# Weighted values of a small attention summed on TensorE instead of VectorE, in pairs of tiles

## The chip, the cores and the metric

The kernel runs on one core of one Trainium2 chip. The metric is the device time of one execution in microseconds; several runs are taken and their median counts. One further execution is recorded by the hardware profiler, and everything said of engines and waits comes from that one.

Engines by the profile's names: PE is TensorE's matmul side and PEld its weight loads, DVE is VectorE, ACT is ScalarE, POOL is GpSimd, SP is SyncE, whose queue issues plain DMAs.

## The reference, cut to what matters

The program is four layers on a residual stream `x` of 4 batches x 1024 tokens x 128 channels. Each layer is half a feed-forward, an attention-like part, and the other half of the feed-forward, each on a layer norm of `x`. In layer 0 the feed-forward is a mixture of 8 experts, of which each token takes the best 2. Its attention does not run over tokens: it runs over the 16 heads of one token.

```python
x = x + 0.5 * _L0_ffn_ref(_layernorm(x), ...)           # experts, top 2 of 8
x = x + _L0_attn_ref(_layernorm(x), Wq, Wk, Wv, Wfc)
x = x + 0.5 * _L0_ffn_ref(_layernorm(x), ...)
...
# _L0_attn_ref, h = 16 heads of hd = 8
scores = einsum('bshd,bstd->bsht', Q, K) / sqrt(hd)     # s: token; h, t: heads
attn = softmax(scores, axis=-1)
out = einsum('bsht,bstd->bshd', attn, V).reshape(b, s, dm)
return out @ Wfc.T
```

For each token that is a 16 x 16 table of scores, a softmax along `t`, and 16 x 8 sums of 16 products with the values.

## The kernel before, in words

The residual stays on chip, channels on the 128 partitions, one tile `X[b]` of 1024 columns per batch. A batch is cut into NT = 8 tiles of 128 tokens. Everything is float32.

**Layer 0's attention** is the generator `l0_attn` (L498 to L569). It first takes the squares and scales of the layer norm (L503 to L511). `projected(i)` (L513) multiplies one tile with the joined weights of q, k and v into a PSUM bank, tokens on the partitions, and ScalarE copies it, scaled per token, into `qkv` (L517). `weighed` (L520) makes, on VectorE, the 128 x 2048 products of q and k for all pairs of heads (L525), sums them over the 8 channels to 256 scores (L527), takes the largest per head (L529) and subtracts it (L530); ScalarE takes the exponential (L532). `summed` (L535) sums the exponentials (L537) and inverts the sums (L538), makes the 2048 products of weights and values (L542), sums them over the 16 positions to 128 outputs (L544) and scales these (L545). The values' weight columns were put in the order (channel, head) on the host (L130), so that L542 and L544 read the positions one after another. TensorE then turns the tile (L562), channels back on the partitions, ScalarE copies it into `oS` (L563), and after four tiles one matmul with `wfc` goes into a bank that VectorE adds to `X` (L567 to L569).

The loop (L549 to L569) runs one tile ahead: the projection two tiles ahead, the scores one tile ahead of the sums.

**What runs beside it.** `experts` (L424) handles a block of 128 tokens of one expert at a time: SyncE's queue loads the weights `e_w` (L455), GpSimd gathers the tokens (L457), TensorE turns them (L461), VectorE copies them (`e_x`, L463), TensorE makes four matmuls, each followed by ScalarE's activation (`e_h`, L468), then four more, VectorE adds the bias (`e_y`, L441), and GpSimd scatters the rows (L442). A group of two batches has 39 blocks, a group of one batch 23. `route` (L276) sorts tokens to experts, with a chain of small VectorE instructions; `combine` (L476) gathers an expert group's results into the residual; `l1_ffn` is the next layer's feed-forward. All matmuls go through the helper `mm`, whose line is L227.

**What sets the order.** Each of these is a generator that yields a cost, in a planner's microseconds. `lanes` (L1182) always advances the lane with the lowest clock; this decides the order in which the program is written down. The attention yields 4 after its norm, 6 after the first scores, and 11.2 per tile; an expert block yields 2.6. Layer 0 is called with three lanes (`macaron`, L1202): one with experts and their routing, one with the attentions of batches 0 to 3 in turn and then the feed-forwards, one with late routing. An attention starts when the first experts of its batch are combined, and the second experts of batches 0 and 1 are routed when the attention of batch 1 is done. From that order the compiler draws up a fixed order for each engine, in which it may let a later instruction pass while an earlier one isn't ready; on the chip each engine then runs its queue in that order.

Tiles come from pools by tag: `qkv` has three buffers, `prod` three, the other tags two. PSUM has a pool of four banks for the expert lane and one of four for the others.

Of the kernel before, what the change touches and what calls it, by code (L numbers as in the profile page):

```python
# [13 lines left out]
ALU = mybir.AluOpType  # L14
AX = mybir.AxisListType

P = 128
B, S, D = 4, 1024, 128
NH, HD = 16, 8
NE, FC = 8, 4  # L20
NT = S // P
# [87 lines left out]
def _col(v):  # L109
    return np.asarray(v).reshape(-1, 1)  # L110


def _moe_pack(w1, w2, b1, b2):

    w2 = w2.reshape(FC, P, NE, D).transpose(1, 2, 0, 3).reshape(P, NE, FC * D)
    b1 = b1.reshape(NE, FC, P).transpose(2, 0, 1)
    return np.concatenate([w1, w2, b1, np.broadcast_to(b2, (P, NE, D))], 2)


def _packs(i):  # L120

    bc = np.broadcast_to

    l0m = [
        ("w", _moe_pack(
            i["L0_ffn_w1"].transpose(2, 0, 1), i["L0_ffn_w2"].transpose(2, 0, 1), i["L0_ffn_b1"], i["L0_ffn_b2"]
        ))
    ]
    l0s = [("rw", i["L0_ffn_router_w"].T)]
    wv = i["L0_attn_Wv"].T.reshape(D, NH, HD).transpose(0, 2, 1).reshape(D, D)  # L130
    l0a = [
        ("wqkv", np.concatenate([i["L0_attn_Wq"].T, i["L0_attn_Wk"].T, wv], 1)),
        ("wfc", i["L0_attn_Wfc"].T),
    ]

    l1f = [
        ("wg", i["L1_ffn_w_gate"].T),
        ("wu", i["L1_ffn_w_up"].T),
        ("wd", i["L1_ffn_w_down"].T.reshape(HIDC, P, D).transpose(1, 0, 2)),
    ]  # L140

    w = i["L1_attn_w_qkv"]
    turned = [2 * d + 1 if d < HD // 2 else 2 * d - HD for d in range(HD)]

    heads = lambda w, order: w.reshape(P, NH, HD)[..., order].reshape(P, D)
    straight = list(range(HD))
    l1a = [
        ("wq", heads(w[:, :D], straight)),
        ("wqt", heads(w[:, :D], turned)),
        ("wk", heads(w[:, D : 2 * D], straight)),  # L150
        ("wkt", heads(w[:, D : 2 * D], turned)),
        ("wv", w[:, 2 * D :]),
        ("wo", i["L1_attn_w_out"]),
        ("bo", _col(i["L1_attn_b_out"])),
    ]

    l2m = [
        ("w", _moe_pack(
            i["L2_ffn_w1"].transpose(1, 0, 2), i["L2_ffn_w2"].transpose(1, 0, 2), i["L2_ffn_b1"], i["L2_ffn_b2"]
        ))  # L160
    ]
# [17 lines left out]
    a = {k[8:]: v for k, v in i.items() if k.startswith("L3_attn_")}  # L179
    at = np.arange(P)  # L180
    turn = at % NH * HD + at // 32 + at % 32 // NH * 4
    l3a = [
        ("maa", np.concatenate([_col(a["time_maa_" + x]) for x in "xwkvrg"], 1)),
        ("w1", a["time_maa_w1"]),
        ("w2", a["time_maa_w2"][:4].reshape(P, D)),
        ("w2l", a["time_maa_w2"][4]),
        ("td", _col(a["time_decay"])),
        ("dw1", a["time_decay_w1"]),
        ("dw2", a["time_decay_w2"]),
        ("u", _col(a["time_faaaa"])),  # L190
        ("wr", a["W_r"]),
        ("wk", a["W_k"]),
        ("wv", a["W_v"][:, turn]),
        ("wg", a["W_g"][:, turn]),
        ("wo", a["W_o"][turn]),
        ("lng", _col(a["ln_gamma"][turn])),
        ("lnb", _col(a["ln_beta"][turn])),
    ]
    return {
        **_constants(),  # L200
        "l0m": l0m, "l0s": l0s, "l0a": l0a, "l1f": l1f, "l1a": l1a,
        "l2m": l2m, "l2s": l2s, "l2a": l2a, "l3f": l3f, "l3a": l3a,
    }


class Macaron:
# [291 lines left out]
    def l0_attn(self, ps, wp, m, b):  # L498
        nc = self.nc
        v = nc.vector  # L500
        X = self.X[b]
        scale = 1.0 / math.sqrt(HD)
        bank = lambda shape=(P, HALF): self.t(ps, list(shape), "bank")  # L503
        sq = self.t(wp, [P, S], "sq", bufs=1)
        for h in range(2):
            c = slice(h * HALF, (h + 1) * HALF)
            cen = bank()
            self.mm(cen, self.c0["center"], X[:, c])
            nc.scalar.activation(sq[:, c], cen, AF.Square)
        r = self.scales(ps, wp, sq, "a")  # L510
        yield 4  # L511

        def projected(i):  # L513
            pq = bank((P, 3 * D))
            self.mm(pq, X[:, i * P : (i + 1) * P], m["wqkvc"])
            qkv = self.t(wp, [P, 3, D], "qkv", bufs=3)
            nc.scalar.mul(qkv.rearrange("p a b -> p (a b)"), pq, r[:, i : i + 1])  # L517
            return qkv

        def weighed(qkv):  # L520
            q = qkv[:, 0, :].rearrange("p (h d) -> p h d", d=HD)
            k = qkv[:, 1, :].rearrange("p (t d) -> p t d", d=HD)
            sh = [P, NH, NH, HD]
            pr = self.t(wp, sh, "prod", bufs=3)
            v.tensor_tensor(pr, q.unsqueeze(2).to_broadcast(sh), k.unsqueeze(1).to_broadcast(sh), ALU.mult)  # L525
            sc = self.t(wp, [P, NH, NH], "sc")
            v.tensor_reduce(sc, pr, AX.X, ALU.add)  # L527
            mx = self.t(wp, [P, NH, 1], "mx")
            v.tensor_reduce(mx, sc, AX.X, ALU.max)  # L529
            v.tensor_tensor(sc, sc, mx.to_broadcast([P, NH, NH]), ALU.subtract)  # L530
            ex = self.t(wp, [P, NH, NH], "ex")
            nc.scalar.activation(ex, sc, AF.Exp, scale=scale)  # L532
            return ex

        def summed(qkv, ex):  # L535
            sm = self.t(wp, [P, NH, 1], "sm")
            v.tensor_reduce(sm, ex, AX.X, ALU.add)  # L537
            v.reciprocal(sm, sm)  # L538
            values = qkv[:, 2, :].rearrange("p (d t) -> p d t", d=HD)
            sh = [P, NH, HD, NH]  # L540
            pv = self.t(wp, sh, "prod", bufs=3)
            v.tensor_tensor(pv, ex.unsqueeze(2).to_broadcast(sh), values.unsqueeze(1).to_broadcast(sh), ALU.mult)  # L542
            o = self.t(wp, [P, NH, HD], "o")
            v.tensor_reduce(o, pv, AX.X, ALU.add)  # L544
            v.tensor_tensor(o, o, sm.to_broadcast([P, NH, HD]), ALU.mult)  # L545
            return o.rearrange("p h d -> p (h d)")


        qkvs = [projected(0), projected(1)]  # L549
        exs = [weighed(qkvs[0])]  # L550
        yield 6
        for i in range(NT):
            if i + 2 < NT:
                qkvs.append(projected(i + 2))
            if i + 1 < NT:
                exs.append(weighed(qkvs[i + 1]))
            k = i % 4
            if k == 0:
                oS = self.t(wp, [P, HALF], "oS")
            o = summed(qkvs[i], exs[i])  # L560
            oT = bank((P, P))
            nc.tensor.transpose(oT, o, self.c0["ident"])  # L562
            nc.scalar.copy(oS[:, k * P : (k + 1) * P], oT)  # L563
            yield 11.2
            if k == 3:
                y = bank()
                self.mm(y, m["wfc"], oS)  # L567
                c = slice((i - 3) * P, (i + 1) * P)
                v.tensor_tensor(X[:, c], X[:, c], y, ALU.add)  # L569


# [774 lines left out]
```

## Time and profile before

| | us |
|---|---|
| median of 3 runs | 3334.71 (3332.87 to 3340.66) |
| the profiled execution | 3264.24 |
| its span, first to last instruction | 3262.4 |
| mean granted TensorE clock | 0.909 |
| layer 0's attention, batch 0 to 3: first product (L525) to last addition (L569), start times | 151.9 to 264.7, 278.8 to 387.9, 413.4 to 539.9, 560.7 to 681.0 |
| VectorE busy, 0 to 955 us | 557.0 |
| TensorE matmul busy, 0 to 955 us | 712.6 |

Three kinds of view are used. The page has the busy share of each engine and cuts the span into 40 equal slices; a digit is the busy share of a slice in tenths, and PEclk the granted TensorE clock in tenths of full speed. A view by windows gives busy microseconds per engine and, in brackets, the number of instructions in each stretch of time. A view by groups puts instructions of one line, operation and shape together: busy us and mean ns of one stand after the bar, then the engine's idle time just before them and what it waited for. Ends of matmuls are modelled and matmuls overlap, so that a sum of their durations is larger than the time that they take; the distance from one to the next is what counts. A float32 matmul appears as two instructions, a transpose as one.

### The profile page before, as it was taken

The numbers are of one execution on the slowest core, as the hardware profiler recorded it, in microseconds if no ns is written. First come the engines' busy times: TensorE is split into PE (matmuls) and PEld (weight loads), VectorE is DVE, ScalarE is ACT, GpSimd is POOL, SyncE is SP. The second block draws the span as 40 slices with busy tenths as digits, with TensorE's granted clock in tenths as the row PEclk, the third lists the DMA queues.
The fourth block names the chain that finished last, engine by engine and source line by source line (L and its number), as shares of the span: only waits on it lengthen the run. The fifth ranks groups of instructions, "written<-read, shape, count | busy, mean of one in ns | idle before, by whom it ended". The sixth has DMA issues, their size and how long they took to land. (4 is left out here: it accounts for less than half of the span.)

```text
span 3262.4 us, 48511 instructions
## 1 busy us (share of the span) xinstructions
PE 2850.0 (87%) x18206; PEld 1660.8 (51%) x18206; DVE 1820.2 (56%) x3156; ACT 1640.6 (50%) x3632; POOL 805.4 (25%) x748
## 2 busy tenths in 40 slices
PE   7777748679879999999999998998988978899997
PEld 6656547556633333333333333586867867334433
DVE  3487786853245775776676771433546521355664
ACT  4556526667404665665565664464433545344442
POOL 2466407433340000000000000064523545010110
PEclk9888959889869999999999998898988989788997
DMA  5655516644400000000000000176644757000000
GB/s 179 193 178 185 168 46 199 183 121 136 152 13 3 6 6 4 6 5 5 17 6 4 1 1 12 47 232 183 200 119 130 217 169 238 13 1 1 7 7 13
DMA packets 122891, 277.64 MB, mean 85 GB/s; under 512 B 18017, under 2 KB 67297, under 8 KB 122529
## 3 DMA queue, kind: packets, MB, share of 16 engines
q1 hardware_dynamic: 101792, 231.77, 23.7%
q0 software_dynamic: 20864, 42.77, 4.2%
q8 instruction: 144, 2.36, 0.3%
q14 instruction: 91, 0.74, 0.1%
HBM read 238.43 MB, written 31.85 MB: 83 GB/s over the span
## 5 line engine op out<-in xcount | busy, mean ns | idle before, releaser
L717 DVE TENSOR_REDUCE nm<-two 128x2 f32<-128x1024 f32 x512 | 626.8, 1224 | 289.9 <-PE s L227 270.5
L740 ACT ACTIVATE e<-s 128x512 f32<-128x512 f32 x1024 | 555.8, 594 | 404.1 <-PE s L227 401.3
L468 ACT ACTIVATE e_h<-bank,e_w 128x128 f32<-128x128 f32 x1304 | 454.6, 368 | 460.9 <-PE bank L227 432.5
L227 PE MATMUL bank<-e_x,e_w 128*128 128x128 f32 x2608 | 560.9, 312 | 110.4 <-DVE e_x L463 43.4
L227 PE MATMUL s<-qm,kz 32*128 32x512 f32 x2048 | 634.2, 643 | 0.8 <-ACT e L740 0.8
L227 PE MATMUL two<-kz,qz 32*128 32x512 f32 x2048 | 593.2, 664 | 19.3 <-DVE nm L717 2.5
L457 POOL DMA_INDIRECT e_xg<-rows,g_source x326 | 336.8, 1033 | 876.8 <-DVE g_target L412 346.6
L227 PEld LDWEIGHTS bank<-e_x,e_w 128*128 128x128 f32 x2608 | 401.8, 197 | 238.1 <-ACT e_h L468 94.7
L442 POOL DMA_INDIRECT res<-e_y,g_target x326 | 369.5, 1134 | 282.9 <-DVE e_y L441 147.8
L227 PE MATMUL bank<-e_w,e_h 128*128 128x128 f32 x2608 | 435.4, 284 | 4.0 <-ACT e_h L468 2.3
L227 PEld LDWEIGHTS bank<-e_w,e_h 128*128 128x128 f32 x2608 | 366.3, 197 | 15.2 <-ACT e_h L468 11.6
L227 PE MATMUL o<-e,va 128*32 128x256 f32 x4096 | 328.6, 392 | 0.1
L441 DVE TENSOR_TENSOR e_y<-bank,e_w 128x128 f32<-128x128 f32 x326 | 94.0, 289 | 386.6 <-PE bank L227 380.5
L227 PEld LDWEIGHTS two<-kz,qz 32*128 32x128 f32 x2048 | 159.6, 189 | 237.8 <-issue 161.3
L227 PEld LDWEIGHTS o<-e,va 128*32 128x32 f32 x4096 | 81.0, 108 | 390.3 <-issue 371.1
L227 PEld LDWEIGHTS s<-qm,kz 32*128 32x128 f32 x2048 | 206.8, 183 | 11.0 <-issue 7.7
L705 POOL COPY va<-vd 128x256 f32<-128x256 f32 x16 | 6.7, 433 | 624.5 <-PE o L227 538.1
L1109 POOL TENSOR_TENSOR z<-st,r 128x512 f32<-128x512 f32 x32 | 46.2, 1444 | 403.3 <-DVE st L1102 240.3
L493 PE MATMUL bank<-c,c_y 128*128 128x128 f32 x128 | 39.3, 450 | 106.2 <-DVE c_y L490 106.2
L463 DVE COPY e_x<-bank 128x128 f32<-128x128 f32 x326 | 92.0, 282 | 62.1 <-PE bank L461 60.3
L461 PE MATMUL bank<-c,e_xg 128*128 128x128 f32 x326 | 93.2, 286 | 7.8 <-DMA e_xg<-rows,g_source 7.7
L227 PE MATMUL bank<-g_cols,g_lanes 128*128 128x39 f32 (+1 forms) x512 | 75.7, 303 | 24.4 <-DVE g_cols L392 24.4
(300 smaller groups left out, 3755.5 us busy)
## 6 DMA issues: line engine op xcount, KB each, us to landing
e_w<-in_l0m_dram SPq DMA_DIRECT2D x170, 578.0 KB
e_w<-in_l2m_dram SPq DMA_DIRECT2D x156, 578.0 KB
c_y<-res SPq DMA_DIRECT2D x32, 512.0 KB
rows<-g_xt SPq DMA_DIRECT2D x16, 512.0 KB
e_xg<-rows,g_source POOLq DMA_INDIRECT x326
res<-e_y,g_target POOLq DMA_INDIRECT x326
x<-in_x_dram SPq DMA_DIRECT2D x4, 512.0 KB
qz<-qd SPq DMA_DIRECT2D x64, 32.0 KB
```

What stands on the lines that cost most here:

```text
L227: self.nc.tensor.matmul(out, lhsT, rhs, start=start, stop=stop)
L441: nc.vector.tensor_tensor(y, o, w[:, MOE_W - D :], ALU.add)
L442: ins = nc.gpsimd.indirect_dma_start(out=res[:, :], out_offset=at(target[:, k : k + 1]), in_=y, in_offset=None)
L457: nc.gpsimd.indirect_dma_start(out=xg, out_offset=None, in_=rows[:, :], in_offset=at(source[:, k : k + 1]))
L461: nc.tensor.transpose(tp, xg, self.c0["ident"])
L463: nc.vector.tensor_copy(x, tp)
L468: nc.scalar.activation(h[:, fc, :], up[:, fc, :], func, bias=w[:, 2 * FC * P + fc : 2 * FC * P + fc + 1])
L493: nc.tensor.transpose(tp[:, j, :], y[1][:, i, :], self.c0["ident"])
L705: nc.gpsimd.tensor_copy(va[n % RING][:, :, :, 1 : 1 + HD], dense[b, "vd"][:, :, 32 * g4 : 32 * g4 + 32].rearrange("p t (h d) -> p t h d", ...
L717: v.tensor_reduce(nm[:, it, h, 2 * pair : 2 * pair + 2], s, AX.X, ALU.max, negate=True)
L740: nc.scalar.activation(es[g], s, AF.Exp, scale=scale)
L1109: (pool if i else v).tensor_tensor(z, st[:, 0:HALF], r, ALU.mult)
```

## The change

The attention of layer 0 is done for two tiles at a time, and the sum over positions moves to another engine.

- `projected` is as before, called for two tiles at a time; `qkv` gets six buffers instead of three. The values keep the order (head, channel).
- `weighed` takes a pair: products and sums of scores tile by tile as before, then the maximum, the subtraction and the exponential once for both tiles, over 512 elements.
- `summed` takes a pair: sum of exponentials and reciprocal once for both, then the exponentials themselves are scaled by it. For each tile VectorE makes the 2048 products, now with the position as outermost index. The sum over positions is 16 matmuls into one PSUM bank: the stationary operand is the 128 x 128 slice of products of a position, the moving operand the identity matrix, and the bank accumulates. The result is at the same time turned, so that the transpose falls away.
- ScalarE copies a pair's result in one instruction of 256 columns.
- The planner's costs become 9 after the scores of a following pair and 8 after the sums of a pair.

```diff
+        def weighed(pair):
+            sc = self.t(wp, [P, 2, NH, NH], "sc")
+            for j, qkv in enumerate(pair):
+                q, k = (qkv[:, n, :].rearrange("p (h d) -> p h d", d=HD) for n in range(2))
...
+                v.tensor_tensor(pr, q.unsqueeze(2).to_broadcast(sh), k.unsqueeze(1).to_broadcast(sh), ALU.mult)
+                v.tensor_reduce(sc[:, j], pr, AX.X, ALU.add)
+            mx = self.t(wp, [P, 2, NH, 1], "mx")
             v.tensor_reduce(mx, sc, AX.X, ALU.max)
+            v.tensor_tensor(sc, sc, mx.to_broadcast([P, 2, NH, NH]), ALU.subtract)
+            ex = self.t(wp, [P, 2, NH, NH], "ex")
             nc.scalar.activation(ex, sc, AF.Exp, scale=scale)
             return ex
...
-            v.tensor_tensor(pv, ex.unsqueeze(2).to_broadcast(sh), values.unsqueeze(1).to_broadcast(sh), ALU.mult)
-            o = self.t(wp, [P, NH, HD], "o")
-            v.tensor_reduce(o, pv, AX.X, ALU.add)
-            v.tensor_tensor(o, o, sm.to_broadcast([P, NH, HD]), ALU.mult)
-            return o.rearrange("p h d -> p (h d)")
+        def summed(pair, ex):
+            sm = self.t(wp, [P, 2, NH, 1], "sm")
             v.tensor_reduce(sm, ex, AX.X, ALU.add)
             v.reciprocal(sm, sm)
+            v.tensor_tensor(ex, ex, sm.to_broadcast([P, 2, NH, NH]), ALU.mult)
+            oT = bank((P, 2, P))
+            for j, qkv in enumerate(pair):
+                values = qkv[:, 2, :].rearrange("p (t d) -> p t d", d=HD)
+                sh = [P, NH, NH, HD]
+                pv = self.t(wp, sh, "prod", bufs=3)
+                v.tensor_tensor(
+                    pv, ex[:, j].rearrange("p h t -> p t h").unsqueeze(3).to_broadcast(sh),
+                    values.unsqueeze(2).to_broadcast(sh), ALU.mult,
+                )
+                for t in range(NH):
+                    self.mm(oT[:, j], pv[:, t].rearrange("p h d -> p (h d)"), self.c0["ident"], start=t == 0, stop=t == NH - 1)
+            return oT
...
+        pairs = [[projected(0), projected(1)]]
+        ex = weighed(pairs[0])
         yield 6
-        for i in range(NT):
...
-            yield 11.2
+        pairs.append([projected(2), projected(3)])
+        for n in range(NT // 2):
+            following = weighed(pairs[n + 1]) if 2 * n + 2 < NT else None
+            yield 9
+            if 2 * n + 4 < NT:
+                pairs.append([projected(2 * n + 4), projected(2 * n + 5)])
...
+            oT = summed(pairs[n], ex)
+            nc.scalar.copy(oS[:, n % 2 * 2 * P : (n % 2 + 1) * 2 * P], oT.rearrange("p i t -> p (i t)"))
+            ex = following
+            yield 8
```

More of the change, by code (lines that the diff above doesn't have):

```diff
@@ L129, in _packs @@
     l0s = [("rw", i["L0_ffn_router_w"].T)]
-    wv = i["L0_attn_Wv"].T.reshape(D, NH, HD).transpose(0, 2, 1).reshape(D, D)
     l0a = [
-        ("wqkv", np.concatenate([i["L0_attn_Wq"].T, i["L0_attn_Wk"].T, wv], 1)),
+        ("wqkv", np.concatenate([i["L0_attn_Wq"].T, i["L0_attn_Wk"].T, i["L0_attn_Wv"].T], 1)),
         ("wfc", i["L0_attn_Wfc"].T),
@@ L515, in projected @@
             self.mm(pq, X[:, i * P : (i + 1) * P], m["wqkvc"])
-            qkv = self.t(wp, [P, 3, D], "qkv", bufs=3)
+            qkv = self.t(wp, [P, 3, D], "qkv", bufs=6)
             nc.scalar.mul(qkv.rearrange("p a b -> p (a b)"), pq, r[:, i : i + 1])
             return qkv
[L520 to L528, printed above, removed]
+        def weighed(pair):
[3 more added lines that the diff above has]
+                sh = [P, NH, NH, HD]
+                pr = self.t(wp, sh, "prod", bufs=3)
+                v.tensor_tensor(pr, q.unsqueeze(2).to_broadcast(sh), k.unsqueeze(1).to_broadcast(sh), ALU.mult)
+                v.tensor_reduce(sc[:, j], pr, AX.X, ALU.add)
+            mx = self.t(wp, [P, 2, NH, 1], "mx")
@@ L529, in weighed @@
             v.tensor_reduce(mx, sc, AX.X, ALU.max)
-            v.tensor_tensor(sc, sc, mx.to_broadcast([P, NH, NH]), ALU.subtract)
-            ex = self.t(wp, [P, NH, NH], "ex")
+            v.tensor_tensor(sc, sc, mx.to_broadcast([P, 2, NH, NH]), ALU.subtract)
+            ex = self.t(wp, [P, 2, NH, NH], "ex")
             nc.scalar.activation(ex, sc, AF.Exp, scale=scale)
             return ex
-        def summed(qkv, ex):
-            sm = self.t(wp, [P, NH, 1], "sm")
+        def summed(pair, ex):
+            sm = self.t(wp, [P, 2, NH, 1], "sm")
@@ L537, in summed @@
             v.tensor_reduce(sm, ex, AX.X, ALU.add)
             v.reciprocal(sm, sm)
[L539 to L542, printed above, removed]
-            o = self.t(wp, [P, NH, HD], "o")
-            v.tensor_reduce(o, pv, AX.X, ALU.add)
-            v.tensor_tensor(o, o, sm.to_broadcast([P, NH, HD]), ALU.mult)
@@ L546, in summed @@
-            return o.rearrange("p h d -> p (h d)")
-        qkvs = [projected(0), projected(1)]
-        exs = [weighed(qkvs[0])]
-        yield 6
-        for i in range(NT):
[L553 to L558, printed above, removed]
-                oS = self.t(wp, [P, HALF], "oS")
[L560 to L563, printed above, removed]
-            yield 11.2
-            if k == 3:
+            v.tensor_tensor(ex, ex, sm.to_broadcast([P, 2, NH, NH]), ALU.mult)
@@ new lines, in summed @@
+            oT = bank((P, 2, P))
+            for j, qkv in enumerate(pair):
+                values = qkv[:, 2, :].rearrange("p (t d) -> p t d", d=HD)
+                sh = [P, NH, NH, HD]
+                pv = self.t(wp, sh, "prod", bufs=3)
[5 more added lines that the diff above has]
+                    self.mm(oT[:, j], pv[:, t].rearrange("p h d -> p (h d)"), self.c0["ident"], start=t == 0, stop=t == NH - 1)
@@ new lines, in summed @@
+            return oT
+        pairs = [[projected(0), projected(1)]]
+        ex = weighed(pairs[0])
+        yield 6
+        pairs.append([projected(2), projected(3)])
[4 more added lines that the diff above has]
+                pairs.append([projected(2 * n + 4), projected(2 * n + 5)])
+            if n % 2 == 0:
+                oS = self.t(wp, [P, HALF], "oS")
+            oT = summed(pairs[n], ex)
+            nc.scalar.copy(oS[:, n % 2 * 2 * P : (n % 2 + 1) * 2 * P], oT.rearrange("p i t -> p (i t)"))
+            ex = following
+            yield 8
+            if n % 2:
@@ L566, in l0_attn @@
                 y = bank()
                 self.mm(y, m["wfc"], oS)
-                c = slice((i - 3) * P, (i + 1) * P)
+                c = slice((n - 1) * 2 * P, (n + 1) * 2 * P)
                 v.tensor_tensor(X[:, c], X[:, c], y, ALU.add)
```

## The prediction

> **What bounds the kernel now.** I read the page first (shares, then slices), next the busy time by stage of layer 0, then the rows of the attention on VectorE, last the pace of single weight loads.
>
> ```profile
> PE 2850.0 (87%) x18206; PEld 1660.8 (51%) x18206; DVE 1820.2 (56%) x3156; ACT 1640.6 (50%) x3632; POOL 805.4 (25%) x748
> ...
> PE   7777748679879999999999998998988978899997
> ...
> DVE  3487786853245775776676771433546521355664
> ...
> PEclk9888959889869999999999998898988989788997
> ```
>
> A slice is 81.6 us. TensorE looks busy overall, but layer 0's attention lies in slices 2 to 8, where VectorE reads 6 to 8 and TensorE often no more. The stages follow from the attention's first and last instructions:
>
> ```profile
> core 0: us, PE busy (x) PEld busy (x) DVE busy (x) ACT busy (x) POOL busy (x), PEclk, DMA share, GB/s
> 143.70:397.00 253.30, 188.87 (x1157) 151.04 (x1155) 196.93 (x287) 154.19 (x352) 151.92 (x117) 0.91 0.58 175
> 397.00:481.00 84.00, 45.87 (x183) 35.34 (x182) 62.06 (x105) 21.93 (x77) 0.00 (x0) 0.56 0.16 54
> 481.00:676.00 195.00, 141.17 (x832) 115.05 (x832) 158.16 (x267) 114.02 (x269) 110.89 (x88) 0.82 0.55 163
> 676.00:955.00 279.00, 233.32 (x1220) 165.81 (x1218) 85.06 (x221) 149.86 (x305) 114.30 (x123) 0.89 0.41 120
> ```
>
> Stage A (143.7 to 397) is the attention of batches 0 and 1 beside the experts, B the routing of batches 0 and 1 beside the attention of batch 2, C the rest of the attention beside experts, D experts and layer 1's feed-forward without attention. DVE fills 78%, 74%, 81% and 30% of them; in 25 us windows inside the attention up to 23.28 of 25 (93%). So A to C wait for VectorE, and these rows of stage A say for what:
>
> ```profile
> L525 DVE TENSOR_TENSOR prod<-qkv 128x2048 f32<-128x2048 f32 x16 | 36.5, 2282 | 0.0
> L527 DVE TENSOR_REDUCE sc<-prod 128x256 f32<-128x2048 f32 x16 | 36.4, 2275 | 0.0
> L544 DVE TENSOR_REDUCE o<-prod 128x128 f32<-128x2048 f32 x16 | 36.3, 2271 | 0.0
> L542 DVE TENSOR_TENSOR prod<-ex,qkv 128x2048 f32<-128x2048 f32 x16 | 35.9, 2245 | 0.0
> ...
> L530 DVE TENSOR_TENSOR sc<-sc,mx 128x256 f32<-128x256 f32 x16 | 6.6, 411 | 0.0
> L537 DVE TENSOR_REDUCE sm<-ex 128x16 f32<-128x256 f32 x16 | 6.5, 409 | 1.4 <-ACT ex L532 1.4
> L529 DVE TENSOR_REDUCE mx<-sc 128x16 f32<-128x256 f32 x16 | 6.5, 407 | 0.0
> L545 DVE TENSOR_TENSOR o<-o,sm 128x128 f32<-128x128 f32 x16 | 4.6, 285 | 0.0
> L538 DVE RECIPROCAL sm<-sm 128x16 f32<-128x16 f32 x16 | 3.9, 243 | 0.0
> ```
>
> The column after the bar is busy us and mean ns, the last the idle time before: next to none. The nine means sum to 10.83 us a tile. Last, the pace of weight loads at full and at half clock, one per matmul record:
>
> ```profile
> 331.71 0.75 PEld L227 LDWEIGHTS bank<-e_w,e_h 128*128 128x128 f32 x6
> ...
> 671.18 1.83 PEld L227 LDWEIGHTS bank<-e_w,e_h 128*128 128x128 f32 x8
> ```
>
> A neighbouring run of 8 at full clock takes 0.97 us, so a record costs (0.97 - 0.75)/2 = 0.11 us; at half clock (1.83 and 1.40 us for 8 and 6) 0.215. A 128x128 f32 matmul has two records: 2608 of them for 326 expert blocks of four. A transpose has one (L562: 32 for 32 tiles).
>
> **What the Trainium skill says.** "FP8 and Floating Point Precision", TensorE Precision Notes: true FP32 takes four passes through the array. The trace agrees in kind: 0.22 us for 128 columns, twice a transpose. "TensorE: Matmul & The Clock Gate", What's actually happening: the clock halves after some 3.4 us of idleness and comes back after as much work. The trace agrees: 0.50 granted in 425 to 475 and in 650 to 675, 1.00 in dense windows. "VectorE: DVE Perf Modes", The perf-mode tier table: fp32 tensor_tensor and tensor_reduce run at 1x only; here 2.25 to 2.28 us for 2048 elements, so only fewer elements or fewer instructions help. "SBUF — State Buffer", Door 1: the DMA port swizzle: reads want at least two hits per 16-byte line. The new product reads ex in steps of 64 bytes, but each value eight times running, so I expect no penalty; no row here has that pattern.
>
> **The change on VectorE.** A pair now costs two products and two sums of scores, 2 x (2.282 + 2.275) = 9.11; three instructions over 512 instead of 256 elements (max, subtraction, sum) at 0.69, as L569 and L399 take for 512: 2.07; the scaling of ex, 0.69; a reciprocal, 0.25; two products with the values, 4.49. Sum 16.61, or 8.31 a tile: 2.52 less, 80.7 us over 32 tiles. What goes is the sum of products (2.27) and half the small instructions; L545 becomes the scaling of ex. Unknown is the product's pattern: at least 2.245; at most the 0.16 us that L364 (256 elements, each a 64-byte step, 0.57) takes over L530, 256 steps in both, so 2.41 or 5 us in all. I take 2.245.
>
> **On TensorE.** 32 tiles x 16 matmuls x 2 records = 1024 records: 112.6 us at full clock (3.52 a tile), 220 at half (6.9). The 32 transposes (3.5 us) go. I take full clock in A and C, since the work itself keeps the clock up; half is the other end. Within B the cost is hidden behind VectorE: even 64 x 0.215 = 13.8 us a pair stays under 16.61. If that cover fails, 3 pairs x 13.8 = up to 41 us.
>
> **On ScalarE.** One exponential per pair, 0.594 instead of 2 x 0.418, and one switch of tables there and back instead of two: up to 16 x 2 x 1.28 = 41 us less. The copies of oS halve in number. ScalarE bounds nothing here (61% in A), so I count zero; expert matmuls wait on e_h (22.1 us in A), so a gain is possible, a loss not. The weights' new order and qkv's six buffers cost nothing in the run; no DMA is moved.
>
> **The order.** The planner's price of a batch falls from 4 + 6 + 8 x 11.2 = 99.6 to 4 + 6 + 4 x 17 = 78, against 2.6 for an expert block: 3.3 blocks are offered per tile instead of 4.3. In the trace about 3 blocks of the next experts run before the attention's end at 676; with attention cheaper they fall into D, where TensorE is full: 3 x 17 records x 0.11 / 0.88 = 6.4, say +6.
>
> **The new wait.** Each group of 32 records stands in TensorE's queue until its product is written. Behind it are expert matmuls, and behind those e_h on ScalarE, e_x and e_y on VectorE. Today the same place costs 15.6 us of idle TensorE (before L562, 32 times).
>
> **The sum.** TensorE's own work, 0.11 per record, 0.32 for 384 columns, 0.43 for 512 (records follow 0.32 and 0.43 apart in the same runs): A has 1111, 32 and 14, together 138.8 us, 55% of 253.3. C has 802, 20 and 10: 98.9, 51% of 195. After: A +16 x 3.52 - 1.8 = 193.3; C, with 13 tiles' products, +45.8 - 1.4 = 143.3. VectorE would need (196.9 - 40.3)/0.93 = 168 and (158.2 - 32.8)/0.93 = 135. So TensorE is late next. What share can it reach? Between 700 and 775, where it is the bound, 337 records at 0.11 and 67 at 0.43 fill 65.9 of 75 us: 88%. With groups that wait for products I take 83%, a choice: A 193.3/0.83 = 232.9 (-20.4), C 143.3/0.83 = 172.7 (-22.3), B 0, D +6. Together -36.7. The profiled execution took 3264.24 us (span 3262.4), so 3227.5; the runs' median lies 70.5 above it, which nothing here explains and which I carry over: 3298.
>
> **Rivals.** (1) More: TensorE reaches 88%, ScalarE's relief feeding it, and D pays nothing: A 219.7, C 162.8, -65.8, so 3269. For it speaks that e_h is the largest wait; against it that no stage with attention comes near. (2) Slower: the queue's wait. If groups stand waiting and experts behind them, and the share stays at 70%, A takes 276.1 (+22.8), C 204.7 (+9.7), D +6: 3373. It decides from a share of 336.6/(448.3 - 6) = 76% downwards. For it: today's 55%, and a clock that may sink during waits; against: products are made in pairs, so the second is ready by the time the first is summed. (3) No change: a share of about 76%, gain and new wait cancel, 3334.
>
> **Chances.** The forecast 0.55 (own range 3278 to 3318: shares 79 to 87%), rival 1 0.17, rival 2 0.20, rival 3 0.08. Faster by over 0.2% (6.7 us, about what a measurement of this kernel can tell from no change) 0.72, same 0.08, slower 0.20. The range 3262 to 3350 leaves out some 0.05 below (all of VectorE's 80.7 saved) and 0.12 above (rival 2's far part, cold clock); the product's pattern (5 us) lies inside.
>
> **What would show it.** L542's successor at 2.25 us and no L544; 1024 records of bank<-prod at 0.11 apart; DVE in A and C down by 40 and 33 us; TensorE's share there near 83%; exponentials' table loads halved; D longer by some 6 us. Wrong if TensorE idles for products, if the granted clock sinks in A or C, or if expert blocks, not attention, end the stages.

## The result: slower by 1.2%, and the profile after

The changed kernel takes 3382.98 us (median of 4 runs, 3380.53 to 3391.79) beside 3337.68 us of the kernel before (4 runs, 3332.87 to 3364.14). The ratio is 1.0121, with a 95% interval from 1.0085 to 1.0157. The forecast was 3298; the time lies above its whole range. A second measurement of both, on another chip, gave 1.0149 (1.0126 to 1.0172).

One caution for all that follows: the same kernel before took about 3358 us on three of the chips used and 3269 on two others; in the comparison above it took 3338, between these. So kernels are compared by their ratio to the kernel before on the same chip, and traces only where the chips are of like pace. The trace behind the prediction (span 3262.4) belongs by its pace to the quicker kind, and the trace after (3390.0) to the slower; where durations are subtracted I use a second trace of the changed kernel (3317.2), which goes with the former, and a second trace of the kernel before (3354.0).

These are the busy times and slices of the changed kernel, to be read against those the prediction shows:

```profile
PE 2968.7 (88%) x19198; PEld 1789.6 (53%) x19198; DVE 1758.7 (52%) x3044; ACT 1614.0 (48%) x3579; POOL 791.8 (23%) x748
...
PE   6788957789778999999999998997987978799997
...
DVE  3385465743224676676677772523445431255664
...
PEclk8898978889976999999999998998987989788997
```

TensorE has 992 records more (1024 came, 32 transposes went). VectorE is busy for 61.5 us less; the attention's rows alone sum to 268 us where they took 32 x 10.83 = 347, so 79 less. Of the 17 us between these two figures some 9 are overlaps, by an estimate: neighbouring instructions overlap by 0.08 us in the records, and there are 112 fewer; the rest I have not traced. Slices 8 to 11, at the end of the attention and after it, show VectorE at 7 4 3 2. The stages, with their ends put where the attention and the expert blocks end in the second trace of the changed kernel (columns: window, its length, busy us and instructions of each engine, granted clock, DMA share, GB/s):

```profile
143.70:409.00 265.30, 233.45 (x1653) 208.81 (x1651) 164.62 (x228) 133.15 (x314) 145.22 (x118) 0.92 0.55 163
409.00:510.00 101.00, 58.29 (x317) 48.87 (x317) 76.03 (x113) 26.79 (x86) 3.45 (x5) 0.67 0.18 57
510.00:692.00 182.00, 157.68 (x1155) 143.66 (x1154) 106.67 (x182) 89.10 (x220) 97.17 (x81) 0.92 0.53 160
692.00:1006.00 314.00, 256.25 (x1264) 179.98 (x1266) 93.73 (x245) 160.82 (x330) 117.84 (x126) 0.84 0.40 115
```

In the first stage VectorE fell from 196.93 to 164.62 us, and the stage still grew from 253.30 to 265.30. The attention itself ended later by only 10.5 us: its last addition into x ends at 692.1 instead of 681.6. The other 40 us came after the attention. From its end to the first rotation in layer 1's attention on VectorE (L685, now L689) it is 240.2 us before (681.6 to 921.8) and 280.6 after (692.1 to 972.7). The new instructions, in the trace after between 140 and 740 us:

```profile
L226 PE MATMUL bank<-c,prod 128*128 128x128 f32 x1024 | 142.2, 285 | 28.7 <-DVE prod L545 27.6 <-issue 1.1
...
L545 DVE TENSOR_TENSOR prod<-ex,qkv 128x2048 f32<-128x2048 f32 x32 | 73.0, 2288 | 3.5 <-PE bank L226 3.2
...
L566 ACT COPY oS<-bank 128x256 f32<-128x256 f32 x16 | 5.9, 371 | 66.3 <-PE bank L226 63.5 <-issue 2.1 <-PE bank L460 0.8
```

The product costs about what was expected (2.288 us where 2.245 was taken), and TensorE waits for products 27.6 us in all. ScalarE's copies wait 63.5 us for TensorE to finish the groups. Where expert blocks run and how fast can be read from e_y on VectorE, one per block. Each window runs from one group's first e_y to its last; the first trace is the kernel before, the second the changed one:

```profile
260.00:388.00 128.00, 10.99 (x39) 55.39 (x39) 0.99 0.65 198
492.00:631.00 139.00, 11.13 (x39) 48.09 (x39) 0.93 0.67 200
```

```profile
267.00:409.00 142.00, 11.26 (x39) 47.67 (x39) 0.94 0.60 179
521.00:686.00 165.00, 11.24 (x39) 46.97 (x38) 0.94 0.56 168
```

The same 39 blocks take 142 us instead of 128, and 165 instead of 139. That is where most of the loss shows.

### The profile page after: what moved, and what is told of

Read it like the earlier page. It is cut to its first block, busy times and chain, and to the rows that moved or that the text cites. A ratio compares the mean times of both kernels' runs of the same rounds, so it can differ in the third digit from the quotient of the medians.

```text
span 3390.0 us, 50356 instructions
## 1 busy us (share of the span) xinstructions
PE 2968.7 (88%) x19198; PEld 1789.6 (53%) x19198; DVE 1758.7 (52%) x3044; ACT 1614.0 (48%) x3579; POOL 791.8 (23%) x748
## 5 line engine op out<-in xcount | busy, mean ns | idle before, releaser
L441 POOL DMA_INDIRECT res<-e_y,g_target x326 | 350.6, 1075 | 283.8 <-DVE e_y L440 170.0
L226 PE MATMUL bank<-c,prod 128*128 128x128 f32 x1024 | 142.2, 285 | 28.7 <-DVE prod L545 27.6
L226 PEld LDWEIGHTS bank<-c,prod 128*128 128x128 f32 x1024 | 131.3, 201 | 31.5 <-DVE prod L545 29.0
L1113 POOL TENSOR_TENSOR z<-st,r 128x512 f32<-128x512 f32 x32 | 46.2, 1444 | 401.7 <-DVE st L1106 240.2
```

The costliest lines, as they stand in the source:

```text
L226: self.nc.tensor.matmul(out, lhsT, rhs, start=start, stop=stop)
L441: ins = nc.gpsimd.indirect_dma_start(out=res[:, :], out_offset=at(target[:, k : k + 1]), in_=y, in_offset=None)
L1113: (pool if i else v).tensor_tensor(z, st[:, 0:HALF], r, ALU.mult)
```

## The experiments

My first theory from the traces was that TensorE's new records were what cost, since a run of 48 of them stands at the end of an attention with VectorE idle. The first rival was that working in pairs at a lower price to the planner costs, the second that the chip or the run made the difference. Each ratio below is to the kernel before on the same chip, with its interval.

**The kernel before again.** No edit.

> The kernel before, unchanged: a second trace of it. If its first profiled execution (3264 us) was merely a fast one, this one comes out near the median of the runs, 3330 to 3345 us, and its attention of batch 0 starts later than 151.9 us, as the changed kernel's does (166). If the low time comes with profiling, this one is near 3264 again. In either case the last sum of products should end within 6 us of each batch's last addition, against some 24 to 40 us in the changed kernel.

Measured: 1.0012 (0.9993 to 1.0031), profiled at 3355.86 us. Its attention of batch 0 starts at 164.7, as the changed kernel's does on a chip of that pace (166.2). So 13 us at the start, and most of the distance between the two first traces, were the chip. The last sum of products ends 3.9 to 6.0 us ahead of each batch's last addition, as expected; in the first trace of the changed kernel 24.1 to 40.0 us lie between the last product and that addition, for TensorE's sum and its wait in the queue come after it.

**Pairs alone, and TensorE's sum alone.** The first puts the reduction, the transpose and the product's old order back into the changed kernel. The second puts the matmuls into the tile-by-tile kernel, with the new product and the exponentials scaled ahead of it. The cuts show the lines that matter.

```
 pairs alone, for each tile of a pair:
-for t in range(NH):
-    self.mm(oT[:, j], pv[:, t]..., ident, start=t == 0, stop=t == NH - 1)
+v.tensor_reduce(o, pv, AX.X, ALU.add)
+nc.tensor.transpose(oT[:, j], o..., ident)
 TensorE's sum alone, in the kernel before:
-v.tensor_reduce(o, pv, AX.X, ALU.add)
-nc.tensor.transpose(oT, o, ident)
+for t in range(NH):
+    self.mm(oT, pv[:, t]..., ident, start=t == 0, stop=t == NH - 1)
```

> The changed kernel with the sum of weighted values back on VectorE (product in the old layout, one reduction, one transpose per tile); pairs, prices and all the rest stay. If TensorE's 1024 records are what costs, this falls to the time before or under it: VectorE has 10.5 us a tile where it had 10.83, so 3325 to 3340. If pairing and the lower prices (fewer expert blocks offered beside the attention) are what costs, it stays slow: 3370 or more.

> The kernel before, tile by tile and with its prices (11.2 a tile), with only the sum over positions moved to TensorE. If TensorE's records cost, it is as slow as the changed kernel or slower, 3375 to 3395, since VectorE saves only 2.1 us a tile here. If pairing and prices cost, it is at 3335 or below.

Measured: pairs alone 1.0120 (1.0093 to 1.0148), TensorE's sum alone 1.0037 (1.0021 to 1.0052). So the first theory does not hold by itself: with TensorE's work as before and nothing but pairs and their price, the whole loss is there. The exchange of VectorE's work for TensorE's costs 0.37% where it stands alone (12 us), less than was expected of it if the records were the cause and more than if they were not. What records cost and what the relief gives is taken apart further below.

**The price.** In the changed kernel, in the one with pairs alone, and by itself in the kernel before:

```
 changed kernel, and pairs alone:
-yield 9      (after weighed)      -yield 8      (after summed)
+yield 12                          +yield 10.4
 kernel before, two kernels:
-yield 11.2
+yield 8.5                         +yield 14
```

> The changed kernel with the attention's price to the planner as it was (12 and 10.4 a pair instead of 9 and 8, 22.4 in all), so that 4.3 expert blocks a tile are offered beside it again. If the lower price made the loss, by blocks that are left over when the attention ends, it gains 20 us or more (3360 or less). If TensorE's records make it, the time stays within 10 us of 3383, since the blocks only change their place on a full engine.

> Pairs with the sum of weighted values on VectorE as in the kernel with pairs only, but with the attention's old price (12 and 10.4 a pair). That kernel was the slowest so far (1.0120 of before) with TensorE's work as before. If the price of 17 a pair, which is too low for 21 us of VectorE work, made that loss, the old price brings it to 0.998 to 1.003 of before. If working in pairs itself costs, it stays above 1.008.

> The kernel before with one number changed: the attention's price is 8.5 a tile (17 for two, as in the changed kernel) instead of 11.2. If the price alone can cost what the change cost, this is 1.008 to 1.014 of before, its expert blocks end later beside the attention and more of them are left for the stages without it. If the price hardly matters, it is within 0.3% of before.

> The kernel before with 14 instead of 11.2 a tile. At 8.5 it lost 1.2%. If more expert blocks ahead of each tile always help, this gains 0.3 to 1%. If 11.2 is where attention and experts end together, this loses too, because attention is then what is left over.

Measured: changed kernel at the old price 1.0075 (1.0050 to 1.0100), pairs alone at the old price 1.0037 (1.0021 to 1.0053), the kernel before at the low price 1.0117 (1.0084 to 1.0149), at the high one 0.9985 (0.9971 to 0.9999). One number, with no instruction added or removed, costs the kernel before as much as the whole change cost. In the changed kernel itself the old price gives back some 0.5 to 0.7% (1.0121 or 1.0149 against 1.0075), so effects overlap: that is 15 to 25 us, about a third to a half of the loss. Pairs at the old price came out just above what was expected if the price made their loss, and the high price gained less than the 0.3 to 1% expected. What the price does shows in the waits during the second group of 39 blocks, first in the kernel before (508 to 659 us), then with the low price (543 to 723). The columns are the waiting engine and line, what it waited for, us in total, times, and the longest:

```profile
ACT e_h L468 <- PE bank L227: 35.7, 61, 2.2
...
PE bank L227 <- ACT e_h L468: 11.6, 21, 1.0
POOL e_xg L457 <- PE bank L227: 11.6, 19, 3.3
```

```profile
POOL e_xg L457 <- PE bank L461: 67.4, 26, 9.7
ACT e_h L468 <- PE bank L227: 59.8, 77, 3.6
...
PE bank L227 <- ACT e_h L468: 33.8, 36, 2.9
```

With the low price TensorE waits for ScalarE's e_h and ScalarE for TensorE, both longer: the two halves of one block wait for each other. As I read it, fewer blocks are at hand between which the engines could alternate; no run shows this apart. The gathers wait 67.4 us until the transposes let a buffer go. The group takes 179 us instead of 150, although the kernels differ in no instruction's work; the granted clock was 0.84 in the one window and 0.89 in the other, and whether that is a cause of the longer waits or follows from them is not shown.

**TensorE's records.** Fifteen of sixteen matmuls left out of the changed kernel:

```
-for t in range(NH):
-    self.mm(oT[:, j], pv[:, t]..., ident, start=t == 0, stop=t == NH - 1)
+self.mm(oT[:, j], pv[:, 0]..., ident)
```

> The changed kernel with one of the 16 matmuls of each tile left (the sum over positions leaves out 15 of 16, so its values are not the reference's): 960 of 1024 records are gone and nothing else. If TensorE's records are paid on the path, it gains the better part of 106 us at full clock, so 60 to 100 (3295 to 3340 beside a before of 3350). If the low price makes the loss, it gains little: under 25 us.

Measured: 1.0013 (0.9992 to 1.0035). Against 1.0121 the 960 records cost 1.1%, some 36 us (22 to 50) of the 106 they take. That lies between the two expectations: TensorE's work is paid, but only about a third of it. In the changed kernel this is no less than what the low price costs it.

**VectorE's relief alone.** The kernel before, tile by tile, with the new product and the same single matmul in place of reduction and transpose:

```
-v.tensor_reduce(o, pv, AX.X, ALU.add)
-nc.tensor.transpose(oT, o, ident)
+self.mm(oT, pv[:, 0]..., ident)
```

> The kernel before, tile by tile at its price, without the reduction of weighted values on VectorE and with nothing in its place: one matmul per tile brings the product of the first position (the other 15 positions are left out). VectorE does 2.1 us a tile less, 68 us in all, TensorE does no more. If VectorE bounds the stages with attention, as the prediction had it, the time falls by 50 to 68 us, to 0.980 to 0.985 of before. If the chain of expert blocks bounds them, it stays within 0.3% of before.

Measured: 0.9923 (0.9899 to 0.9947), 26 us (18 to 34) for 68 us of VectorE work. This is neither of the two expectations: it counts, at 0.38 us for one. The trace says where it does not count. Beside the first 39 blocks the attention of batch 1 ends at 365.4 us instead of 405.3 in the second trace of the kernel before, 40 us sooner, and the blocks end at 397.4 instead of 404.0, under 7 us sooner; routing follows the blocks and their sums in both (its scores g_l at 428.0 and 436.7).

TensorE's sum alone (1.0037) against this one prices the records a second time: 1.1%, 38 us (29 to 48). These two kernels have the same price and steps and differ by 960 records. Their second groups of 39 blocks, first without the records, then with them, as windows (columns as in the view by stages) and as waits of the block's steps for TensorE:

```profile
501.00:652.00 151.00, 122.84 (x760) 107.35 (x760) 102.18 (x194) 95.37 (x229) 90.47 (x74) 0.88 0.58 182
...
DVE e_y L440 <- PE bank L226: 34.4, 28, 6.0
ACT e_h L467 <- PE bank L226: 27.4, 51, 1.5
...
DVE e_x L462 <- PE bank L460: 9.9, 4, 4.5
```

```profile
520.00:683.00 163.00, 140.05 (x998) 125.25 (x997) 96.02 (x194) 93.99 (x226) 85.61 (x75) 0.94 0.54 169
...
ACT e_h L467 <- PE bank L226: 46.1, 75, 1.9
...
DVE e_y L440 <- PE bank L226: 33.4, 21, 4.0
...
DVE e_x L462 <- PE bank L460: 10.3, 8, 3.5
```

With the records the waits for TensorE are 89.8 us instead of 71.7, and the group takes 12 us longer. The granted clock is higher with them, 0.94 against 0.88, and so it is in the changed kernel, 0.92 with sixteen matmuls a tile against 0.86 with one. So part of what the records take may come back through faster matmuls around them; the runs do not separate how much.

**No attention.** All its instructions in layer 0 left out of the kernel before, the planner's steps kept:

```
-weighed(...), summed(...), projected(...) and what follows them
+yield 4; yield 6; eight times yield 11.2
```

> The kernel before with every instruction of layer 0's attention left out, the planner's steps and prices kept: what the experts, routing and sums of layer 0 take by themselves. If attention on VectorE sets the end of its stages (253 and 195 us), the experts alone leave a good half of them: 150 us or more below before (0.955 or less). If the expert blocks set it, at 3.3 to 3.9 us a block with or without attention, the time falls by less than 60 us (0.982 or more).

Measured: 0.9650 (0.9621 to 0.9678), 117 us less, between the two expectations. The 39-block groups of this kernel, to be held against 130 and 150 us of the kernel before on a chip of like pace:

```profile
250.00:367.00 117.00, 11.37 (x39) 37.42 (x38) 0.96 0.67 217
450.00:577.00 127.00, 11.08 (x38) 37.53 (x38) 0.89 0.66 213
```

The expert blocks need most of their time with or without an attention beside them: 115 us for 39 blocks, 3.0 a block, where it is 3.4 beside the attention. All attention together, 32 times 10.83 = 347 us of VectorE, costs only 117.

**What holds the expert blocks.** Six buffers for their weights, and about half the transfers of weights (88 instead of 170 in layer 0), both in the kernel before:

```
-w = self.t(wp, [P, MOE_W], "e_w", bufs=4)
+w = self.t(wp, [P, MOE_W], "e_w", bufs=6)
 the other kernel:
+if k % 2 == 0 or func != AF.Gelu:
     w = self.t(wp, [P, MOE_W], "e_w", bufs=4)
     nc.sync.dma_start(out=w, in_=weights[...])
```

> The kernel before with six buffers for the experts' weights instead of four (layers 0 and 2). In the traces the queue of loads waits for a buffer until an e_y on VectorE has read its bias. If that ring sets the pace of the expert blocks, this gains 1% or more; if the transfers themselves do (578 KB a block), or TensorE, under 0.3%.

> The kernel before with the weights of layer 0's experts loaded for every second block only; the block between uses the weights loaded before it, so the values are not the reference's. If the transfers of 578 KB set the pace of the expert blocks (at 3.0 to 3.3 us a block they need 175 to 195 GB/s), layer 0 falls by 60 us or more, to 0.982 or less. If TensorE and the steps from engine to engine set it, the time stays within 0.5% of before.

Measured: six buffers 0.9974 (0.9961 to 0.9987), half the loads 1.0009 (0.9996 to 1.0022). Transfers do not set the pace, and the ring of buffers does so only a little. What is left, from engine to engine within a block and TensorE's records, I have not taken apart further.

**Finer steps.** The changed kernel at the old price, with a step after every tile of a pair:

```
 in weighed and summed, after the first tile of the pair:
+if j == 0:
+    yield 6       (weighed)       +    yield 5.2     (summed)
 in the loop:
-yield 9                           -yield 8
+yield 6                           +yield 5.2
```

> The changed kernel at the attention's old price, with a step for the planner after every tile's products and sums (6, 6, 5.2, 5.2) where there were two to a pair (12, 10.4), so that expert blocks are offered four times a pair. If long stretches of one lane make what is left of the loss at the old price (1.0075), it falls to 1.004 or below, the level of the kernel without pairs. If TensorE's work makes it, it stays at 1.006 to 1.009.

Measured: 1.0004 (0.9984 to 1.0025), against 1.0075 for the same price in two steps. Smaller portions between offers of expert blocks are worth 0.7%.

**Half of the sum on each engine, and the better forms.** With fine steps, once with the sum shared, once with a higher price and five weights' buffers, once with all of these; and the kernel before with its own price and buffers bettered:

```
 shared sum:
+v.tensor_tensor(pv[:, 0:8], pv[:, 0:8], pv[:, 8:16], ALU.add)
-for t in range(NH):
+for t in range(8):
 price and buffers with fine steps:
-yield 6 / yield 5.2               -"e_w", bufs=4
+yield 7 / yield 7                 +"e_w", bufs=5
 kernel before:
-yield 11.2                        -"e_w", bufs=4
+yield 14                          +"e_w", bufs=6
```

> The changed kernel at the old price with fine steps (1.0004), with the sum shared: VectorE adds positions 8 to 15 to 0 to 7 in one instruction of 1024 elements, TensorE sums eight. VectorE does some 1.15 us a tile more (37 us), TensorE 512 records less (56 us at full clock). By the slopes of the runs so far (0.38 us for one of VectorE, 0.36 for one of TensorE) this costs 14 and gains 20: 0.998 of before, hardly told from 1.0004. If VectorE is the bound it loses 20 us or more (1.006); if TensorE is, it gains as much (0.990).

> The changed kernel with fine steps, 7 a step (28 a pair, 14 a tile) and five buffers for the experts' weights. If what the change loses is the order alone, it ends below before by what price and buffers gave the kernel before (0.15% and 0.26%): 0.993 to 0.997. If TensorE's records still cost more than VectorE's relief gives, it stays at 0.999 to 1.004.

> The kernel before at 14 a tile with six buffers for the experts' weights, the two edits that gained 0.15% and 0.26% by themselves. If they add up, 0.996; if both only shift the same waits, 0.998. It is what the changed kernel's best form has to be held against.

> The changed kernel with fine steps, the sum shared between VectorE (one addition of 1024 elements) and TensorE (eight matmuls a tile), 7 a step and five weights' buffers. The shared sum had 0.9968, price and buffer 0.9964 without it, against 1.0004 for fine steps alone: if the gains add up, 0.992 to 0.994, the fastest form here. If both only fill the same idle places, 0.996 to 0.998.

Measured: shared sum 0.9968 (0.9955 to 0.9980), price and buffers with fine steps 0.9964 (0.9948 to 0.9980), the kernel before with both edits 0.9968 (0.9953 to 0.9983), all together 0.9880 (0.9858 to 0.9903). The last is the fastest of the kernels that do all the work, 3232.52 us beside 3269.46, and it gains more than the parts let expect. Sharing the sum gains 0.36% over fine steps alone, 12 us where the two slopes let 6 be expected. With order and buffers bettered on both sides, the sum on TensorE (0.9964) and the sum on VectorE (0.9968) cannot be told apart; only the shared sum is clearly faster. The groups of 39 blocks in the fastest form:

```profile
257.00:381.00 124.00, 11.21 (x39) 46.66 (x38) 0.99 0.67 200
488.00:610.00 122.00, 11.21 (x39) 42.55 (x37) 0.99 0.74 227
```

Here 39 blocks beside the attention take 122 us where the kernel before takes 139 and the changed kernel 165. A group's own time is not the whole of it, though: with price and buffers but without the shared sum the second group takes only 109 us, and then 58 us pass to the next group's first e_y, where 35 pass here. That group ran at a granted clock of 1.00; the one without attention took 126 at 0.89.

**The changed kernel again.**

> The changed kernel once more, unaltered, beside before on whichever chip comes. If the loss lies in the order of the work, fixed when the kernel is built, it comes out at 1.008 to 1.016 again, on a faster chip too. If it came from that chip or those four runs, it is within 0.5% of before.

Measured: 1.0149 (1.0126 to 1.0172). The loss is the program's.

## Why the prediction was wrong

**What bounds the kernel.** The prediction said that stages A to C wait for VectorE. This is the step that failed. VectorE was 93% busy in some windows and had next to no idle time ahead of its attention rows, and both only say that there was always attention work to fill it. What set the time was mostly the chain of routing, expert blocks and sums, which runs from 55 us to the end of layer 0 and which the attention delays. The run with the relief alone shows it for stage A: attention that ended 40 us sooner brought the end of the blocks under 7 us nearer. Late in stage C the attention does count: in the same run the second group of 39 is as long as before and ends 7.5 us sooner (651.8 instead of 659.3), and the next group begins 18.6 us sooner (683.6 instead of 702.2). The prediction named it as what would make it wrong ("if expert blocks, not attention, end the stages"), and the changed kernel shows it: in its second trace the attention of batch 1 ends at 386.4 and the 39 blocks beside it at 407.7. In the kernel before both ended together (388.6 and 387.1), so one view of ends could not tell them apart. The pace of blocks could have hinted at it: in 700 to 775 us, without attention though beside layer 1's feed-forward, the kernel before made 16 blocks in 75 us (with one pause of 14 us for a sum), no faster than beside it. Taking the attention out altogether saves 117 us, of 347 us of VectorE's work.

Along that chain, in us between e_y of the named groups (the first two columns on the quicker chips, the next three on the slower ones, the last on a quicker one):

| | before | changed | before | before at 8.5 | no attention | all edits together |
|---|---|---|---|---|---|---|
| 23 blocks of batch 1 | 87.7 | 91.9 | 87.9 | 94.8 | 66.8 | 80.8 |
| 39 blocks of batches 2, 3 | 126.9 | 140.6 | 130.5 | 147.0 | 115.0 | 123.0 |
| to the next group (routing) | 105.1 | 113.5 | 104.9 | 113.8 | 84.2 | 108.0 |
| 39 blocks of batches 0, 1 | 138.0 | 164.3 | 150.4 | 179.2 | 126.4 | 120.9 |
| from there to the last block | 237.5 | 227.9 | 247.4 | 242.2 | 239.7 | 237.7 |

The changed kernel and the kernel before at the low price lose in the same places, and above all in the second group of 39.

**VectorE's saving** was right in size: the product at 2.288 us lies between the bounds of 2.245 and 2.41, and the attention's rows fell by 79 us where 80.7 were expected. Of the Trainium skill, "SBUF — State Buffer", Door 1, the reading holds: steps of 64 bytes cost 0.04 us where each value is read eight times running. Its worth was wrong: the stages were let shrink with VectorE until TensorE took over, which left 42.7 us of gain in A and C after all of TensorE's added work; the run with the relief alone gains 26 us for 68, with no work added.

**TensorE's cost** was right in size, a run of 48 records takes 5.44 us, 0.113 apiece, and the clock stayed up as the prediction had it (0.92 granted in the first and third stage), in line with the same skill's "TensorE: Matmul & The Clock Gate", What's actually happening. That TensorE would be "late next" at a chosen share of 83% was no sound step: its own 193.3 us in stage A are 73% of the 265.3 measured. Records cost 0.36 us for one although TensorE's own work is far below a full share. In the second group of 39 the waits of the block's steps for TensorE grew; first the kernel before, then the changed one:

```profile
ACT e_h L468 <- PE bank L227: 31.7, 59, 1.3
DVE e_y L441 <- PE bank L227: 20.1, 14, 6.9
...
DVE e_x L463 <- PE bank L461: 7.4, 4, 2.7
```

```profile
ACT e_h L467 <- PE bank L226: 49.2, 74, 3.9
...
DVE e_y L440 <- PE bank L226: 39.8, 23, 2.9
DVE e_x L462 <- PE bank L460: 20.5, 11, 4.6
```

They grew from 59.2 to 109.5 us, and the group by 26. This is not the records' doing alone: the low price by itself raises the same three waits from 72.3 to 99.6 us. The pair of kernels that differ by the records only has 71.7 and 89.8, so longer waits within a block are shown for them too, but smaller.

**The order** is the second term that was mis-sized. The exchange of VectorE's work for TensorE's stood in the sum at -42.7 us and is +12 where it was run alone; the order stood at +6. The prediction saw the price fall from 99.6 to 78 and counted three blocks. The time after the attention grew by 40. In the kernel before the second group of 39 blocks ends at 630, and the wait for their results and the sums that follow (43 us to the next e_y) lie beside the last 51 us of attention; in the changed kernel the group ends at 685.5, 6.6 us ahead of the attention's end, and the same wait (38 us) has nothing beside it. The low price by itself costs the kernel before 1.17% (39 us), and in the changed kernel 15 to 25 us.

**The sum with the measured terms:** relief -26, records +36 to +38, price +39 in the kernel before; together +49 to +51, where 45 (1.2%) and 49 (1.5%) were measured. That they add up so closely is partly luck: each term is uncertain by 8 to 14 us, the price weighs less in the changed kernel (0.5 to 0.7%) and pairs at the old price cost 0.37% by themselves, which is not in this sum.

**The other points.** The new wait in TensorE's queue, which carried rival 2 (3373, the nearest number), was not the cause: TensorE waits 27.6 us for products, where it waited 15.6 before, and the kernel with one position, whose single matmuls wait 31.1 us for the same products, is at 1.0013. So rival 2 had the direction and not the mechanism. ScalarE's relief came (table loads at the exponential from 26 to 14, at e_h from 56 to 45, 29.5 us together); what it bought no run shows. Taking the profile's own time for the sum and carrying the 70 us to the median did no harm: the trace's pace is that of a quicker chip, and the ratio was the same there or larger.

What stays open: how much of a block's 3.0 us is TensorE's and how much the way from engine to engine; how much of each loss goes through the granted clock; and why pairs at the old price still cost 0.37% when finer steps take that and more away. That the size of the portions does it was shown for the changed kernel only. Why all edits together gain more than each, I did not settle either.

## What to carry to other kernels

An engine that is always busy beside a long chain need not be the bound: take the chain's own pace from a place without the busy engine's work, ask how much shorter the chain would be there, and look which of the two ends later when the engine is relieved. Where a planner orders the work by prices, a price changed along with the work is an edit of its own; test it alone, since here one number moved the kernel before as much as the whole change did. Work moved between two engines that both serve the chain was worth about a third of its length here on either side (0.38 and 0.36 us for one), so moving it lost where it became longer, 68 us on VectorE against 106 on TensorE.

## What the runs showed of the hardware that I had not expected

The chips differ: the same program took 3358 us (three chips) and 3269 us (two), 2.7% apart, while ratios between kernels repeated within their intervals (1.0121 and 1.0149). Leaving out 82 of the 170 transfers of layer 0's weights (578 KB each, 98 MB in all) changed nothing (1.0009), although the core moves 160 to 200 GB/s in those stages; in the fastest form it moved 227. An addition of 1024 elements on VectorE, both operands and result in one tile, takes 1.21 us, a little over half of a product of 2048 (2.28). With work added to TensorE the granted clock around it was higher: 0.86 without and 0.92 with it in the second group of 39 of the changed kernel, 0.88 and 0.94 in that of the kernel before, for 960 records.
